# An fp32 latent-attention and mixture-of-experts layer: order of scores, mixing and statistics around the pairs

## The chip, the cores and the metric

The kernel runs on one core of one Trainium2 chip. The metric is device time of one execution in microseconds (us); the time given is the median of several runs.

## The reference

All numbers are fp32. `x` holds 32 batches of 32 latent rows of 512 values (1,024 rows); `ctx` holds 32 batches of 257 context rows of 384 values.

```python
h = LN(LN(x), g1, b1); c = LN(ctx, g2, b2)
q = h @ Wq + bq; k = c @ Wk + bk; v = c @ Wv + bv       # cross-attention, per batch
x = x + softmax(q @ k.T / sqrt(512)) @ v @ Wo + bo
h = LN(x)                                                # self-attention, per batch
q, k, v = three projections of h in 16 heads of 32 values; q, k = rope(q), rope(k)
x = x + concat(softmax(q @ k.T / sqrt(32)) @ v) @ Wo2.T + bo2
y = LN(x)
scores = sigmoid(y @ gate.T + bias)                      # 8 experts
share = the two best scores of a row / (their sum + 1e-6)
x = x + sum over the two of share * (silu(y @ w1[e].T) @ w2[e].T)
```

(Shortened: the kernel folds the key and value projections into the query and output weights, so that the context's normalisation reaches the scores as a factor per context row, the `rs` and `rx` below.)

## The kernel before

128 rows make a tile; there are eight tiles (groups, `g`) of four batches each, and four pairs of tiles (`p`). TensorE takes its instructions in the order in which the program is written. On VectorE (DVE), ScalarE (ACT) and GpSimd (POOL) a scheduler orders them by its own reckoning of when each can start; `tc.issue_after(x)` holds an instruction back until `x` in that reckoning. Each engine executes its own list in order. SyncE (SP) issues the loads and stores; POOL issues the indirect scatters.

The stages, with the profile's times:

1. Folding of weights (0 to 45 us).
2. Cross-attention, a loop over nine steps (45 to 139 us). A step `g` does `xmix_turn(g-1)` (transposes of the weights `ex`, tile `pte`, copied by ACT to `eT`, L628), `xscores(g)` (`pscore`, L580), `xmix(g-1)` (`pc` L637, then on DVE the mix `u`, L644), `xweights(g)` (transposes `prs` of the spread row factors `rx`, L595; scores times factors, exponentials), `cstats(g+1)` (eight `bn_stats` L528 on DVE, then `inverse` L510 to L518 on POOL, the last step a power that gives `rs`), `rspread(g+1)` (`rx`, an ACT copy, L564), `xout_turn(g-1)` (`ptu` L662), the queries of the next pair (`pq` L483 evacuated by ACT to `q2T` L487; `pbt` L475, copied to `pbs` L480, then `pb` L492), and `xout(g-1)` (`po` L671, residual sum L674). `cstats(g)` is held until the mix `u` of `g-2` (`pace["c", g]`).
   `load_ctx` brings the rows `n` of a group three steps ahead. Behind the last of them SP issues the four attention weights, and then a fill of `xs_d`, the experts' list in memory, with zeros (8 writes of 2,112 KB, L170).
3. Self-attention by pairs (139 to 303 us). For each pair: `scores` (`pqs`, 128 matmuls of 32 by 32, then maximum, subtraction and exponential), `shares` (sum, reciprocal, product, transposition into `aT`), `attend` (`pos`, 128 matmuls of 32 by 32, evacuated as `oT` L922, then `ppo` L934), `norm2`, the gate's logits, and for the pair before it `pick` (two best experts and shares) and `places` (positions in the experts' lists, `pi` L1068, and four scatters L1072 of rows to `xs_d`). `project` and `rotate` of the next pair lie between. `norm`, `xnorm` and `norm2` make `rs` by POOL's power and `nb`, minus mean times `rs`, on DVE.
   The last pair (250 to 303 us) has no next pair; `values(3,1)` (`ppv`), the sort of the experts by load (`order`) and the first expert's early work (`xse`, loaded from `xs_d` when the first three pairs' scatters have landed; transposes `xpe`, first matmuls `phe`) fill it.
4. The experts (303 to 540 us).

The order of the self-attention loop's start and of the last pair's start, before:

```python
# pair p of the loop (p = 0: no picks)
project(p + 1, 0, 0); shares(p, 0); scores(p, 1)
# picks of p - 1
project(p + 1, 0, 1); shares(p, 1); rotate(p + 1, 0); attend(p, 0)
project(p + 1, 1, 0); step(norm, p + 2); attend(p, 1)
# last pair
pick(p - 1); scores(p, 1); places(p - 1); values(p, (1,)); order(); attend(p, 0)
```

Of the kernel before, what the change touches and what calls it, by code (L numbers as in the profile page):

```python
# [1 line left out]

# [7 lines left out]
F32 = mybir.dt.float32  # L10
# [3 lines left out]
ALU = mybir.AluOpType  # L14
# [3 lines left out]
P = 128  # L18
# [34 lines left out]
def tile_perceiver_layer(  # L53
# [172 lines left out]
    with ExitStack() as attn:  # L226
# [19 lines left out]
        with ExitStack() as xa:  # L246
# [80 lines left out]
            def room(p, tag):  # L327
# [7 lines left out]
                    rooms[i // 4] = ewp.tile([P, KF * D], F32, tag="ew", name=f"pair{i // 4}")  # L335
                return rooms[i // 4][:, ts(i % 4, KD * N2)]

            def normalized(p, dsts):

                mv = spool.tile([P, 2, 2], F32, tag="mv2", name="mv2")  # L340
                for i in range(2):
                    stats_of(x_sb[:, 2 * p + i, :], mv[:, i, :])
                rs = rstd_of(mv, 2)
                nb = spool.tile([P, 2], F32, tag="nb", name="nb")
                nc.vector.scalar_tensor_tensor(
                    nb, mv[:, :, 0], -1.0, rs, op0=ALU.mult, op1=ALU.mult
                )
                for i in range(2):
                    nc.scalar.activation(
                        dsts[i], x_sb[:, 2 * p + i, :], AF.Identity,  # L350
                        bias=nb[:, i : i + 1], scale=rs[:, i : i + 1],
                    )
# [68 lines left out]
            def xnorm(p):  # L421

                mv = spool.tile([P, 2, 2], F32, tag="mv2", name="mv2")
                with tc.issue_after(pace["x", p]):
                    for i in range(2):
                        stats_of(x_sb[:, 2 * p + i, :], mv[:, i, :])

                ve = spool.tile([P, 2], F32, tag="ve2", name="ve")
                nc.vector.tensor_scalar(
                    ve, mv[:, :, 1], 1.0 + EPS, EPS * EPS, ALU.mult, ALU.add  # L430
                )
                rs = spool.tile([P, 2], F32, tag="rs2", name="rs")
                nc.gpsimd.tensor_tensor(rs, ve, mhalf[:, :2], ALU.pow)
                nb = spool.tile([P, 2], F32, tag="nb", name="nb")
                nc.vector.scalar_tensor_tensor(
                    nb, mv[:, :, 0], -1.0, rs, op0=ALU.mult, op1=ALU.mult
                )
                y = wk.tile([P, 2, D], F32, tag="y", bufs=1, name="y")
                for i in range(2):
                    nc.scalar.activation(  # L440
                        y[:, i, :], x_sb[:, 2 * p + i, :], AF.Identity,
                        bias=nb[:, i : i + 1], scale=rs[:, i : i + 1],
                    )
                qs[p]["y"] = y
# [61 lines left out]
            def inverse(st, m, n, tag):  # L506


                d = spool.tile([P, m], F32, tag="d" + tag, bufs=2, name="d9")[0:n]
                nc.gpsimd.tensor_tensor(d, st[:, :, 1], st[:, :, 4], ALU.subtract)  # L510
                nc.gpsimd.tensor_tensor(d, d, d, ALU.mult)
                v = spool.tile([P, m], F32, tag="v" + tag, bufs=2, name="v9")[0:n]
                nc.gpsimd.tensor_tensor(v, st[:, :, 2], st[:, :, 5], ALU.add)
                nc.gpsimd.tensor_scalar(d, d, DC / 4.0, EPS * DC, ALU.mult, ALU.add)
                nc.gpsimd.tensor_tensor(v, v, d, ALU.add)
                nc.gpsimd.tensor_scalar(v, v, 1.0 / DC, 0.0, ALU.mult, ALU.add)
                rs = spool.tile([P, m], F32, tag="rs" + tag, bufs=2, name="rs9")[0:n]
                nc.gpsimd.tensor_tensor(rs, v, mhalf[0:n, :m], ALU.pow)  # L518
                return rs

            def cstats(g):

                n = gs[g]["n"]
                st = spool.tile([P, 8, 6], F32, tag="st9", bufs=2, name="st9")

                with tc.issue_after(pace["c", g]):
                    for r in range(8):
                        nc.vector.bn_stats(st[:, r, :], n[:, r // 2, r % 2, :])  # L528
                gs[g]["rs"] = inverse(st, 8, P, "9")

            def lstats():
# [10 lines left out]
                nc.vector.tensor_reduce(  # L542
                    own[:, NTT:], eye.rearrange("p g b -> p b g"), AX.X, ALU.add
                )
                nc.vector.tensor_scalar_mul(own[:, 0:NTT], own[:, 0:NTT], rs)
                nc.vector.tensor_copy(
                    to.rearrange("p (b q) -> p b q", q=T),
                    own[:, NTT:].unsqueeze(2).to_broadcast([4 * NTT, 4, T]),
# [11 lines left out]
            def rspread(g):  # L560

                rs = gs[g]["rs"]
                rx = wk.tile([P, 2, 4, T], F32, tag="rx", bufs=1, name="rx")
                nc.scalar.copy(  # L564
                    rx,
                    rs[:, 0:8].rearrange("p (b c) -> p c b", c=2)
                    .unsqueeze(3).to_broadcast([P, 2, 4, T]),
                )
                rb = wk.tile([P, S], F32, tag="rb", name="rb")
                nc.scalar.copy(rb[:, NK : NK + 1], rlast[:, g : g + 1])  # L570
                gs[g]["rx"], gs[g]["rb"] = rx, rb
# [95 lines left out]
            def xout(g):  # L667
                uT = gs[g]["uT"]
                po = ps.tile([P, D], F32, tag="ps", name="po")
                for c in range(KC):  # L670
                    nc.tensor.matmul(  # L671
                        po, uT[:, c, :], wvo[:, c, :], start=(c == 0), stop=(c == KC - 1)
                    )
                nc.vector.scalar_tensor_tensor(  # L674
                    x_sb[:, g, :], po, gs[g]["rc"], x_sb[:, g, :],
                    op0=ALU.mult, op1=ALU.add,
                )


            DX = DC + 1  # L680
# [152 lines left out]
        with ExitStack() as sa:  # L833
# [16 lines left out]

            scatters = []
            cums = []
            def values(p, tiles=(0, 1)):
                for i in tiles:
                    v = wk.tile([P, D], F32, tag="v", bufs=4, name="v")
                    pp = ps.tile([P, D], F32, tag="ps", name="ppv")
                    for k in range(KD):
                        nc.tensor.matmul(  # L858
                            pp, st[p]["yT"][:, k, ts(i, P)], av[:, k, :],
                            start=(k == 0), stop=(k == KD - 1),  # L860
                        )
                    nc.scalar.copy(v, pp)
                    st[p]["v", i] = v

            def scores(p, i):

# [2 lines left out]
                for k in range(KD):  # L869
# [10 lines left out]
                mx = spool.tile([P, 4, KD], F32, tag="smx", name="smx")  # L880
                nc.vector.tensor_reduce(mx, sv, AX.X, ALU.max)
                ex = wk.tile([P, NH, T], F32, tag="sex", bufs=3, name="sex")
                nc.vector.tensor_tensor(
                    ex.rearrange("p (m k) s -> p m k s", k=KD),
                    sv,
                    mx.unsqueeze(3).to_broadcast([P, 4, KD, T]),
                    ALU.subtract,
                )
                nc.scalar.activation(ex, ex, AF.Exp, scale=ASCALE)
                st[p]["ex", i] = ex  # L890

# [97 lines left out]
            def pick(p):  # L989
# [25 lines left out]
                    )  # L1015
                nc.gpsimd.tensor_tensor(cc[:, 1, :], cc[:, 0, :], mk[:, 0, :], ALU.add)
                cums.append((cc, mk))

                sg = rt.tile([P, 2, 2], F32, tag="sg2", name="sg2")
                if p == NP - 1:  # L1020
                    nc.scalar.activation(sg, top[:, :, 0:2], AF.Sigmoid)
                else:
                    en = rt.tile([P, 2, 2], F32, tag="en", name="en")
                    nc.scalar.activation(en, top[:, :, 0:2], AF.Exp, scale=-1.0)
                    nc.vector.tensor_scalar_add(en, en, 1.0)
                    nc.vector.reciprocal(sg, en)
                den = rt.tile([P, 2], F32, tag="den", name="den")
                nc.vector.reduce_sum(den, sg, axis=AX.X)
# [7 lines left out]
                for i in range(2):  # L1036
# [3 lines left out]
                        y[:, i, YC : YC + NE], m[:, i, 1, :], c2[:, i, 1:2], cb,  # L1040
                        op0=ALU.mult, op1=ALU.add,
                    )
                st[p]["m"], st[p]["mk"], st[p]["cc"] = m, mk, cc

            def places(p):

                y, m, mk, cc = st[p]["fy"], st[p]["m"], st[p]["mk"], st[p]["cc"]
# [48 lines left out]
                nc.vector.tensor_copy(c, pn[:, 0:NE])  # L1096
                return c

            def order():

                full = [P, NE, NE]
                c = counts(cums[-1], "cnt0")
                key = keep.tile([P, NE], F32, name="key")
                nc.vector.scalar_tensor_tensor(
                    key, c, float(NE), down, op0=ALU.mult, op1=ALU.add
# [118 lines left out]
            def step(f, p, *a):  # L1224
                if 0 <= p < NP:
                    f(p, *a)
# [4 lines left out]
            for p in range(NP - 1):  # L1231
# [3 lines left out]
                    gate_turn(p - 1, 1)  # L1235
                project(p + 1, 0, 0)
                shares(p, 0)
                scores(p, 1)
                if p:
                    gate_logits(p - 1, 0)  # L1240
                    gate_logits(p - 1, 1)
                    pick(p - 1)
                project(p + 1, 0, 1)
                shares(p, 1)
                rotate(p + 1, 0)
                attend(p, 0)
                project(p + 1, 1, 0)
                step(norm, p + 2)
                attend(p, 1)
                if p:  # L1250
                    places(p - 1)
                project(p + 1, 1, 1)
                rotate(p + 1, 1)
                finish(p, 0)
                norm2(p, 0)
# [14 lines left out]
            shares(p, 0)  # L1270
            pick(p - 1)
            scores(p, 1)
            places(p - 1)
            values(p, (1,))
            order()
            attend(p, 0)
            shares(p, 1)
            finish(p, 0)
            norm2(p, 0)
# [8 lines left out]
            early_hidden(1)  # L1288
            gate_logits(p, 1)
            pick(p)  # L1290
            early_hidden(2)
            places(p)
            cnt = counts(cums[-1], "cnt")
# [343 lines left out]
```

## Time and profile before

| what | value |
|---|---|
| median of 9 runs | 552.15 us (550.63 to 556.8) |
| profiled execution | 551.48 us, span 549.8 us, mean granted TensorE clock 0.992 |
| TensorE busy | 515.4 us |
| VectorE busy | 242.2 us |
| ScalarE busy | 123.4 us |
| GpSimd busy | 105.9 us |
| DMA | 104.56 MB, mean 190 GB/s |

The profile is one execution. Busy time of TensorE is modelled from the starts of its matmuls. A row of the slices shows the span in 40 equal parts, each digit a busy share in tenths. A row of the waits names the waiting engine, tile and line, what released it, and the idle microseconds before it. A row of the timeline gives start, length, engine, line, operation, tiles (out<-in), and in brackets the idle time of the engine just before it with its releaser; "issue" there is idle time in which nothing that the profile shows was waited for.

### The profile page before, as it was taken

What the parts mean: (1) busy time and instruction counts of PE and PEld (TensorE: products, weight loads), DVE (VectorE), ACT (ScalarE), POOL (GpSimd) and SP (SyncE); (2) the same over time, 40 slices, a digit from 0 to 9 for tenths busy, and PEclk for the clock granted to TensorE, in tenths of its full rate; (3) what the DMA queues carried; (4) which work ended last, traced back from release to release, by engine and by line L of the source; (5) the groups of instructions that cost most, each with busy time, mean ns of one, the idle gap of its engine ahead of it and who ended that gap; (6) DMA issues with size and microseconds to landing.
All of it is one profiled execution on the core that took longest, in us unless ns stands there. A gap on an engine that the chain in (4) does not pass through costs nothing. (4 is left out here: it accounts for less than half of the span.)

```text
span 549.8 us, 11309 instructions
## 1 busy us (share of the span) xinstructions
PE 515.4 (94%) x4718; PEld 335.1 (61%) x4718; DVE 242.2 (44%) x706; ACT 123.4 (22%) x274; POOL 105.9 (19%) x185
## 2 busy tenths in 40 slices
PE   6999998999989999999899899999999999999991
PEld 3655454556665784876476366557566574868571
DVE  6564668655686575678651232113122121313110
ACT  3444444322311412312131021002011020102010
POOL 2323445220000013021302200131211202111202
PEclk9999999999999999999999999999999999999996
DMA  7999997999951002011594240936574436646512
GB/s 262 392 383 387 312 312 266 333 390 386 386 185 40 3 4 117 4 55 67 207 396 168 37 155 14 332 93 181 166 229 140 127 117 176 204 165 201 167 20 29
DMA packets 43647, 104.56 MB, mean 190 GB/s; under 512 B 4001, under 2 KB 7233, under 8 KB 42562
## 3 DMA queue, kind: packets, MB, share of 16 engines
q1 hardware_dynamic: 38994, 94.96, 48.3%
q0 software_dynamic: 4592, 8.78, 7.9%
q8 instruction: 39, 0.64, 0.5%
q14 instruction: 22, 0.18, 0.1%
HBM read 75.55 MB, written 28.18 MB: 189 GB/s over the span
## 5 line engine op out<-in xcount | busy, mean ns | idle before, releaser
L1402 PE MATMUL ph<-xT,w 128*128 128x288 f32 (+4 forms) x448 | 100.2, 382 | 3.1 <-ACT xT L177 3.1
L1402 PEld LDWEIGHTS ph<-xT,w 128*128 128x128 f32 x448 | 79.0, 190 | 19.6 <-ACT xT L177 3.7
L1464 PE MATMUL fpo<-w,hT 128*128 128x512 f32 x192 | 84.3, 595 | 0.0
L1464 PEld LDWEIGHTS fpo<-w,hT 128*128 128x128 f32 x192 | 35.9, 190 | 43.7 <-issue 43.5
L1408 DVE TENSOR_TENSOR hT<-ph,sg 128x288 f32<-128x288 f32 (+4 forms) x56 | 23.6, 422 | 62.9 <-ACT sg L1407 62.8
L1469 DVE TENSOR_SCALAR fob<-fpo,share 128x512 f32<-128x512 f32 x12 | 9.0, 751 | 76.5 <-PE fpo L1464 76.5
L1407 ACT ACTIVATE sg<-ph 128x288 f32<-128x288 f32 (+4 forms) x56 | 21.5, 384 | 85.0 <-PE ph L1402 81.3
L195 POOL DMA_INDIRECT out_dram<-fob,idx x12 | 18.6, 1548 | 103.2 <-DVE fob L1469 93.3
L528 DVE BATCH_NORM_STATS2 st<-n 128x6 f32<-128x384 f32 x64 | 32.7, 544 | 0.7 <-DMA n<-in_ctx_dram 0.6
L195 POOL DMA_INDIRECT out_dram<-fob,plc x9 | 13.9, 1547 | 91.6 <-DVE fob L1374 74.9
L177 ACT COPY xT<-xpt 128x512 f32<-128x512 f32 (+2 forms) x12 | 6.0, 497 | 112.5 <-PE xpt L1384 112.4
L934 PE MATMUL ppo<-ao,oT 128*128 128x512 f32 x64 | 28.5, 595 | 2.4 <-DVE oT L922 2.4
L671 PE MATMUL po<-wvo,uT 128*128 128x512 f32 x48 | 22.4, 602 | 1.2 <-ACT uT L664 1.2
L483 PE MATMUL pq<-x1T,mq 128*128 128x256 f32 x96 | 23.0, 384 | 0.0
L1072 POOL DMA_INDIRECT xs_d<-fy,pi x16 | 17.0, 1060 | 30.1 <-DVE pi L1068 20.2
L388 PE MATMUL pp<-syT,ak 128*128 128x256 f32 x96 | 22.4, 385 | 0.0
L1369 PE MATMUL fpq<-w,hT 128*32 128x128 f32 (+1 forms) x576 | 22.3, 309 | 0.0
L388 PE MATMUL pp<-syT,aq 128*128 128x256 f32 x96 | 22.1, 383 | 0.0
L934 PEld LDWEIGHTS ppo<-ao,oT 128*128 128x128 f32 x64 | 12.0, 190 | 15.8 <-issue 12.9
L858 PE MATMUL ppv<-av,syT 128*128 128x512 f32 x48 | 21.3, 594 | 0.0
L1369 PEld LDWEIGHTS fpq<-w,hT 128*32 128x32 f32 x576 | 16.3, 110 | 7.1 <-issue 3.2
L483 PEld LDWEIGHTS pq<-x1T,mq 128*128 128x128 f32 x96 | 17.4, 190 | 3.6 <-issue 1.2
(280 smaller groups left out, 734.1 us busy)
## 6 DMA issues: line engine op xcount, KB each, us to landing
xs_d<-zero SPq DMA_DIRECT2D x8, 2112.0 KB, 20.4
w<-in_w1T_dram SPq DMA_DIRECT2D x16, 1024.0 KB, 8.3
w<-in_w2T_dram SPq DMA_DIRECT2D x16, 1024.0 KB, 8.1
nT<-in_ctxT_dram SPq DMA_DIRECT2D x8, 1542.0 KB, 9.4
n<-in_ctx_dram SPq DMA_DIRECT2D x32, 384.0 KB, 7.2
xs<-xs_d SPq DMA_DIRECT2D x4, 528.0 KB, 9.2
x_sb<-in_x_dram SPq DMA_DIRECT2D x8, 256.0 KB, 6.6
out_dram<-x_sb SPq DMA_DIRECT2D x8, 256.0 KB, 2.9
```

The source lines that it names most:

```text
L195: return nc.gpsimd.indirect_dma_start(out=dst, out_offset=bass.IndirectOffsetOnAxis(ap=place, axis=0), in_=ob, in_offset=None, bounds_chec ...
L388: nc.tensor.matmul(pp[:, i, :], w[:, k, ts(e, P)], yT[:, k, :], start=(k == 0), stop=(k == KD - 1),)
L483: nc.tensor.matmul(pq[:, 0 : 2 * P], mq[:, k, ts(c, P)], x1T[:, k, :], start=(k == 0), stop=(k == KD - 1),)
L528: nc.vector.bn_stats(st[:, r, :], n[:, r // 2, r % 2, :])
L671: nc.tensor.matmul(po, uT[:, c, :], wvo[:, c, :], start=(c == 0), stop=(c == KC - 1))
L858: nc.tensor.matmul(pp, st[p]["yT"][:, k, ts(i, P)], av[:, k, :], start=(k == 0), stop=(k == KD - 1),)
L934: nc.tensor.matmul(pp, st[p]["oT", i][:, k].rearrange("p b q -> p (b q)"), ao[:, k, :], start=(k == 0), stop=(k == KD - 1),)
L1369: nc.tensor.matmul(po[ts(g, Q), 0:w], hT[:, f, ts(h, Q)], w2[:, f, ts(j, w)], start=(f == 0), stop=(f == KF - 1),)
L1402: nc.tensor.matmul(ph[:, 0:n], w1[:, k, ts(f, P)], t["xT"][:, k, 0:n], start=(k == 0), stop=(k == KD - 1),)
L1407: nc.scalar.activation(sg[:, 0:n], ph[:, 0:n], AF.Sigmoid)
L1408: nc.vector.tensor_mul(hT[:, f, 0:n], ph[:, 0:n], sg[:, 0:n])
L1464: nc.tensor.matmul(po, hT[:, f, ts(c, P)], w2[:, f, :], start=(f == 0), stop=(f == KF - 1),)
```

## The change

Five edits:

1. A helper `offsets` makes `nb` in `normalized` and `xnorm`: DVE negates the mean in place, POOL multiplies it by `rs`. Before, DVE did both in one instruction that read POOL's `rs`.
2. `inverse` loses its step `v * 1/DC`; the factor `DC ** 0.5` goes into the products that read `rs` (`own` on DVE, `rx` on ACT, now `nc.scalar.mul`).
3. In `cstats(g)` for `g >= 4`, three of the eight `bn_stats` are held only until the residual sum of `xout(g-3)`, and no longer until the mix of `g-2`.
4. First pair: `scores(0,1)` stands behind one more `project`, `attend(0,0)` and `attend(0,1)` each behind one more.
5. Last pair: `pick` is split in `pick` and `pick_shares`; the shares follow the second scores, and their first DVE step is held until the second subtraction. `values(3,1)` is split in halves; `places`, `counts` and `attend(3,0)` come between them, `order` behind them.

```diff
+            def offsets(mv, rs):
+                less = mv[:, :, 0]
+                nc.vector.tensor_scalar_mul(less, less, -1.0)
+                nb = spool.tile([P, 2], F32, tag="nb", name="nb")
+                nc.gpsimd.tensor_tensor(nb, less, rs, ALU.mult)
+                return nb
...
-                nb = spool.tile([P, 2], F32, tag="nb", name="nb")
-                nc.vector.scalar_tensor_tensor(
-                    nb, mv[:, :, 0], -1.0, rs, op0=ALU.mult, op1=ALU.mult
-                )
+                nb = offsets(mv, rs)
...
-                nc.gpsimd.tensor_scalar(v, v, 1.0 / DC, 0.0, ALU.mult, ALU.add)
...
-                with tc.issue_after(pace["c", g]):
-                    for r in range(8):
+                for r in range(8):
+                    soon = g >= 4 and r < 3
+                    with tc.issue_after(pace["r" if soon else "c", g]):
                         nc.vector.bn_stats(st[:, r, :], n[:, r // 2, r % 2, :])
...
-                nc.vector.tensor_scalar_mul(own[:, 0:NTT], own[:, 0:NTT], rs)
+                nc.vector.tensor_scalar(
+                    own[:, 0:NTT], own[:, 0:NTT], rs, DC ** 0.5, ALU.mult, ALU.mult
+                )
...
-                nc.scalar.copy(
+                nc.scalar.mul(
                     rx,
                     rs[:, 0:8].rearrange("p (b c) -> p c b", c=2)
                     .unsqueeze(3).to_broadcast([P, 2, 4, T]),
+                    DC ** 0.5,
                 )
...
-                nc.vector.scalar_tensor_tensor(
+                pace["r", g + 3] = nc.vector.scalar_tensor_tensor(
                     x_sb[:, g, :], po, gs[g]["rc"], x_sb[:, g, :],
                     op0=ALU.mult, op1=ALU.add,
-                )
+                ).ins
...
+            def pick_shares(p):
+                y, m, top = st[p]["fy"], st[p]["m"], st[p]["top"]
...
-                    nc.vector.tensor_scalar_add(en, en, 1.0)
+                    late = st[NP - 1].get(("less", 1))
+                    with tc.issue_after(late) if late else nullcontext():
+                        nc.vector.tensor_scalar_add(en, en, 1.0)
...
                 shares(p, 0)
-                scores(p, 1)
                 if p:
+                    scores(p, 1)
                     gate_logits(p - 1, 0)
                     gate_logits(p - 1, 1)
                     pick(p - 1)
+                    pick_shares(p - 1)
                 project(p + 1, 0, 1)
+                if p == 0:
+                    scores(p, 1)
                 shares(p, 1)
                 rotate(p + 1, 0)
-                attend(p, 0)
+                if p:
+                    attend(p, 0)
                 project(p + 1, 1, 0)
+                if p == 0:
+                    attend(p, 0)
                 step(norm, p + 2)
-                attend(p, 1)
                 if p:
+                    attend(p, 1)
                     places(p - 1)
                 project(p + 1, 1, 1)
+                if p == 0:
+                    attend(p, 1)
...
             pick(p - 1)
             scores(p, 1)
+            pick_shares(p - 1)
+            values(p, (1,), range(0, 2))
             places(p - 1)
-            values(p, (1,))
-            order()
+            n = counts(cums[-1], "cnt0")
             attend(p, 0)
+            values(p, (1,), range(2, KD))
+            order(n)
             shares(p, 1)
```

More of the change, by code (lines that the diff above doesn't have):

```diff
@@ L1 @@
-from contextlib import ExitStack
+from contextlib import ExitStack, nullcontext
 import concourse.bass as bass
@@ L433, in xnorm @@
                 nc.gpsimd.tensor_tensor(rs, ve, mhalf[:, :2], ALU.pow)
-                nb = spool.tile([P, 2], F32, tag="nb", name="nb")
-                nc.vector.scalar_tensor_tensor(
-                    nb, mv[:, :, 0], -1.0, rs, op0=ALU.mult, op1=ALU.mult
-                )
+                nb = offsets(mv, rs)
                 y = wk.tile([P, 2, D], F32, tag="y", bufs=1, name="y")
@@ L673, in xout @@
                     )
-                nc.vector.scalar_tensor_tensor(
+                pace["r", g + 3] = nc.vector.scalar_tensor_tensor(
                     x_sb[:, g, :], po, gs[g]["rc"], x_sb[:, g, :],
                     op0=ALU.mult, op1=ALU.add,
-                )
+                ).ins
             DX = DC + 1
@@ L852, in tile_perceiver_layer, with values @@
             cums = []
-            def values(p, tiles=(0, 1)):
+            def values(p, tiles=(0, 1), ks=range(KD)):
                 for i in tiles:
-                    v = wk.tile([P, D], F32, tag="v", bufs=4, name="v")
-                    pp = ps.tile([P, D], F32, tag="ps", name="ppv")
-                    for k in range(KD):
+                    if ks[0] == 0:
+                        st[p]["pv", i] = ps.tile([P, D], F32, tag="ps", name="ppv")
+                    pp = st[p]["pv", i]
+                    for k in ks:
                         nc.tensor.matmul(
@@ L861, in values @@
                         )
-                    nc.scalar.copy(v, pp)
-                    st[p]["v", i] = v
+                    if ks[-1] == KD - 1:
+                        v = wk.tile([P, D], F32, tag="v", bufs=4, name="v")
+                        nc.scalar.copy(v, pp)
+                        st[p]["v", i] = v
             def scores(p, i):
@@ L882, in scores @@
                 ex = wk.tile([P, NH, T], F32, tag="sex", bufs=3, name="sex")
-                nc.vector.tensor_tensor(
+                st[p]["less", i] = nc.vector.tensor_tensor(
                     ex.rearrange("p (m k) s -> p m k s", k=KD),
@@ L887, in scores @@
                     ALU.subtract,
-                )
+                ).ins
                 nc.scalar.activation(ex, ex, AF.Exp, scale=ASCALE)
@@ L1017, in pick @@
                 cums.append((cc, mk))
+                st[p]["m"], st[p]["mk"], st[p]["cc"], st[p]["top"] = m, mk, cc, top
+            def pick_shares(p):
+                y, m, top = st[p]["fy"], st[p]["m"], st[p]["top"]
                 sg = rt.tile([P, 2, 2], F32, tag="sg2", name="sg2")
@@ L1042, in pick @@
                     )
-                st[p]["m"], st[p]["mk"], st[p]["cc"] = m, mk, cc
             def places(p):
@@ L1097, in counts, with order @@
                 return c
-            def order():
+            def order(c):
                 full = [P, NE, NE]
-                c = counts(cums[-1], "cnt0")
                 key = keep.tile([P, NE], F32, name="key")
@@ L1290, in tile_perceiver_layer @@
             pick(p)
+            pick_shares(p)
             early_hidden(2)
```

## The prediction

> **What bounds the kernel now.** I read the page's busy times first, then the slices, then the waits of TensorE, and only then the timelines of the three places that the change touches.
>
> ```profile
> PE 515.4 (94%) x4718; PEld 335.1 (61%) x4718; DVE 242.2 (44%) x706; ACT 123.4 (22%) x274; POOL 105.9 (19%) x185
> DMA  7999997999951002011594240936574436646512
> ```
>
> TensorE is busy for 94% of the span, so nothing here can save much except by closing holes in its row. The DMA row says which holes may be tied to transfers: the 16 engines are full from the start to about 157 us, then nearly idle.
>
> ```profile
> PE prs L595 <- ACT rx L564: 4.0, 3, 1.4
> PE ppo L934 <- DVE oT L922: 2.4, 2, 1.6
> PE ptu L662 <- DVE u L644: 1.3, 2, 0.9
> PE pqs L873 <- issue: 1.2, 1, 1.2
> PE pos L915 <- issue: 0.9, 1, 0.9
> PE pmc L746 <- ACT trow L740: 0.6, 1, 0.6
> PE pr L1050 <- DVE sg L1026: 0.5, 1, 0.5
> ```
>
> Each line is: waiting matmul, what released it, us in total, times, longest. All seven are within the change's reach; together they are 10.9 us (2.0% of the span). That is the ceiling; the rest of the prediction asks how much of it is really collected. The experts' stage, 303 to 540 us, issues the same instructions in the same order before and after; I cost it at nothing, and so are the middle pairs, where the split of pick leaves the order as it was.
>
> **First pair: second scores and mixing behind projections (pqs, pos).**
>
> ```profile
> 152.29 0.55 PE L873 MATMUL pqs<-pair 32*32 32x32 f32 x41
> 154.01 0.94 PE L873 MATMUL pqs<-pair 32*32 32x32 f32 x87 [1.17 <-issue]
> 158.53 0.32 PE L915 MATMUL pos<-aT,v 32*32 32x32 f32 x25
> 159.74 1.07 PE L915 MATMUL pos<-aT,v 32*32 32x32 f32 x103 [0.89 <-issue]
> ```
>
> Columns: start, length, engine and line, then the idle time before it. In both groups of 128 small matmuls TensorE stops in the middle, for "issue", with all its data there. From the first stop to the second there are 87 small matmuls, 16 wide ones and 25 small ones: 128, each with its weight load, so 256 instructions. The instruction queue (q8 on the page) moves 16 KB packets at 151.45, 157.26 and 160.84, so a stop every 256 instructions is TensorE running out of code. Two groups of 128 tiny matmuls (10 ns each) use up a block in 1.3 us, while the zero fill of xs_d (its last landing is 160.29) holds the DMA engines that must bring the next one. In the changed order each group of small matmuls has one more wide group (16 matmuls, 3.72 us) ahead of it. The next block is then due 25 small matmuls into the second scores, at about 156.2, where before it was there by 154.0, and the one after it 9 into the first mixing, at about 161.0, when the fill has ended. So both stops should go: 1.17 + 0.89 = 2.06 us. If the second block is asked for at 156.4 and takes the 5.9 us that the one before took (148.0 to 154.0), it comes at 162.3, and up to 1.0 us of the second stop stays; with the DMA row falling to 3 and then 0 tenths there I keep 0.15. Term: **-1.9 us** (bounds -2.1 and 0).
>
> [...]
>
> **Cross-attention: statistics ahead of the mix, one POOL step less.** In inverse() one TENSOR_SCALAR goes; POOL's steps start 0.28 us apart (78.20 to 78.48), so every rs comes 0.28 us sooner. Twice in a row (lstats, then cstats(0)) that gives 0.56 of the 0.60 us that pmc waits for trow, which stands on ACT behind the first rx: -0.5 us. The first long wait of prs (71.53, 1.32 us) belongs to group 3, whose statistics don't move: -0.25.
>
> For groups 4 to 7 three of eight bn_stats (0.49 us apart, 1.46 together) go ahead of the mix's u, and the rest no longer stand behind the product of ex (0.4 to 0.6 us): rs comes 1.8 to 2.6 us sooner with the POOL step, I take 2.3 (rx becomes an ACTIVATE; q2T, an ACTIVATE of the same size, takes 0.47 where the copy took 0.40, which I count within this). But look at what ACT does with it:
>
> ```profile
> 75.79 0.47 ACT L487 ACTIVATE q2T<-pq,tcol 128x256 f32<-128x256 f32 x1
> 76.39 0.37 ACT L480 COPY pbs<-pbt 128x256 f32<-128x256 f32 x1
> 80.15 0.40 ACT L564 COPY rx<-rs 128x256 f32<-128x256 f32 x1 [3.39 <-POOL rs L518]
> 89.97 0.37 ACT L628 COPY eT<-pte 128x256 f32<-128x256 f32 x1 [0.37 <-PE pte L626]
> 93.59 0.40 ACT L564 COPY rx<-rs 128x256 f32<-128x256 f32 x1 [3.26 <-POOL rs L518]
> ```
>
> Now rx is last of its group and waits 3.39 us behind q2T and pbs. In the changed kernel, as it is built, rx stands ahead of q2T and pbs for groups 4 and 6, and ahead of eT for groups 5 and 7, because the scheduler reckons it ready sooner. ACT takes its instructions in order, so these copies wait for rx, and TensorE for them:
> - Group 4: rx at 80.15 - 2.3 = 77.85; q2T 0.31 later, pbs ends 0.84 after that, 79.0. The matmul pb ran at 78.08 without a wait, so it now waits about 1.1 us (0.2 of it is TensorE's own lead). +1.1.
> - Group 6: rx 102.91 - 2.3 = 100.6, pbs done at 101.75, pb was at 100.61: +1.0 after the lead.
> - Group 5: rx 91.3, eT done at 91.95, so pc starts at 92.05 instead of 91.18; prs follows it at 93.5 where it ran at 94.05 after its wait of 1.40: -0.5. The same for group 7 (rx 115.26, prs 115.71 after 1.33): -0.45.
> - nb: DVE no longer waits for POOL's pow (2.10 us at 94.26, 0.81 at 82.14, the latter followed by an nb of 1.23 us where others take 0.16). This is what ptu's 0.89 us comes from (u stood behind it): -0.4 of it, since u now has three bn_stats ahead of it instead (1.46 us, partly where the wait was). The price is eight POOL products of 0.2 us, right behind pow, and eight DVE products of 0.16 us; ACT's y and pair start at most 0.1 us later, beside a TensorE that has pq and po to do.
>
> Sum: -0.5 - 0.25 + 1.1 + 1.0 - 0.5 - 0.45 - 0.4 = **0.0 us**. The uncertain size is how much sooner rs comes; every 0.1 us of it is worth about 0.4 us over four groups (bounds -4.4 with rx out of the way, +2.8 if it gains 0.7 us less).
>
> On that nb of 1.23 us: it began at 82.14, beside a POOL addition that began at 82.07 and took 1.26. [...]
>
> **Last pair: shares behind the scores, mixing between.**
>
> ```profile
> 262.73 0.17 DVE L1068 CAST pi<-place 128x4 int32<-128x4 f32 x1
> 263.69 1.06 POOL L1072 DMA_INDIRECT xs_d<-fy,pi  x1 [3.53 <-DVE ssm L895]
> 276.46 0.22 DVE L1186 COPY_PREDICATED_SCALAR pl<-mask,xse 128x1 int32 x1 [2.67 <-DMA xse<-xs_d]
> ```
>
> TensorE waits here 0.45 (pr for sg), 0.81 and 1.56 (the two ppo for oT), 2.8 us in all, with the first mixing held up by two small gaps (1.84 us instead of 1.29). After the change attend(3,0) runs before the second half of values(3,1), so oT has 1.9 us of matmuls to hide in, its POOL scatters no longer lie across the mixing, and en + 1 stands behind the second subtraction, so the score chain (subtraction at 261.48) starts about 1.0 us sooner. Up to the second ppo that is 2.0 us. But pi, which every scatter reads, now comes behind the shares, counts and the keys of the order (some ten operations of 0.1 to 0.2 us, less the 0.68 us subtraction): about 0.6 us later. The scatters keep the 0.8 us from pi's end to their start, so xse lands at 277.05 instead of 276.45. The transposes xpe, which ran at 277.39 right behind ppo, would be due at 275.4 and wait until 277.15; gained so far 0.25. Behind them x_sb and its statistics are already done (they stood at 277.59 and 278.31, ahead of DVE's half of the copy xTe at 278.92), so that half comes 0.5 to 0.7 us sooner and phe, which waited 0.48, with it. Term: **-0.7 us** (bounds -2.0, xse no later, and +0.4, pi 1.2 us later).
>
> **Sum.** 0.0 - 1.9 - 0.7 = -2.6 us. The profiled execution took 551.48 us (span 549.8 and 1.7 around it), so its like would take 548.9; the median of the nine runs is 0.67 above it: 552.15 - 2.6 = **549.5 us**. What this kernel's measurement can tell from no change is about 0.5%, 2.76 us, so the forecast lies on that border.
>
> **Rivals.**
> - A, rx comes in time: rs gains over 3 us, and neither pb nor pc waits. Then the waits of prs go too (1.40 + 1.33), and with -0.5, -0.25, -0.9 the stage gives -4.4: 552.15 - 4.4 - 1.9 - 0.7 = 545.2. For it: rs's chain behind the last bn_stats is only 3.2 us. Against: five of eight bn_stats still follow u. Chance 0.12.
> - B, slower: rx blocks ACT for longer. Each us that rs comes later than I think costs 4 us (two pb, two pc). With rs only 1.65 us sooner instead of 2.3 the whole gain is gone; with 0.95 us sooner the time is 552.15 + 2.8 = 555. It decides where bn_stats in front of u wait on DVE for their rows n, which are in a saturated queue (n takes 7.2 us to land, up to 13.9). Chance 0.09.
> - C, the stops travel: TensorE runs dry in the new places as well, first-pair term zero: 551.4. For it: the fill's end is only 0.7 us before the second need. Chance 0.14.
> - D, the last pair's xse eats all, or the keys come earlier than I think: 550.2 or 548.2, inside the forecast's own range.
>
> **Numbers.** My forecast, with D in it, has 0.65, with a range of its own of 547.6 to 551.2, about half of it below 549.4. Faster by over 0.5%: 0.12 from A and 0.35 of the 0.65; slower by over 0.5%: half of B and a little for what no row shows, 0.08; between them 0.45. For 8 in 10 the low end goes part of the way to A (546.5), the high end past C to where B begins (552.5).
>
> **What would show it.** Right: no "issue" wait in pqs and pos of the first pair; prs no longer in the list, but pb and pc waiting for ACT pbs and eT, about 1 us each; xpe waiting for xse. Wrong: rx starting at once on ACT (then A), pb's waits of 2 us and more (B), a stop inside pqs or pos (C), xpe without a wait (last pair worth 2 us).

## The result, and the profile after

The changed kernel takes 559.15 us (median of 10 runs, 555.73 to 562.13), against 552.05 us of the kernel before beside it: ratio 1.012, 95% interval [1.0092, 1.0147]. I had forecast 549.5, with a range of 546.5 to 552.5. Its profiled execution has a span of 555.5 us, 5.7 more than before, and a mean granted clock of 0.985 (before 0.992). The medians lie 7.1 us apart; the other 1.4 us are in no trace. One run, of e7 below, took 1073.28 us and is left out of its ratio, though not of its median.

Waits of TensorE in the changed kernel, those that bear on the change, to be held against the seven lines shown before (waiting matmul, releaser, us in total, times, longest):

```profile
PE xpe L1197 <- DMA xse<-xs_d: 4.0, 1, 4.0
PE pc L643 <- ACT eT L634: 2.3, 3, 1.1
PE pb L494 <- ACT pbs L482: 1.9, 2, 1.0
PE pos L924 <- issue: 1.8, 1, 1.8
PE ppo L943 <- DVE oT L931: 1.6, 1, 1.6
PE prs L601 <- ACT rx L569: 1.0, 1, 1.0
PE ptu L668 <- DVE u L650: 0.7, 2, 0.4
PE pp L393 <- issue: 0.4, 1, 0.4
```

Of the seven waits that were named, those of prs, ppo and ptu are smaller and those of pqs, pmc and pr are gone; the stop of pos for issue, 1.8 us where it was 0.9, and the waits for xse, eT and pbs stand in their place. Pieces of TensorE's own time line show where the time went: the first matmuls of the self-attention begin at 146.66 (before 146.46, +0.2); the second pair's at 185.01 (182.90, +2.1); the last pair's second scores at 259.87 (257.95, +1.9); the first expert's transposes xpt at 317.78 (310.85, +6.9). From there on both kernels run alike. (The end of the span is 5.7 us later; 1.2 us are made up behind the last matmul.) So the cross-attention came out as forecast, the first pair lost 1.9 us where I had 1.9 as a gain, and the last pair lost 5.0.

In the cross-attention rx stands ahead of q2T and pbs on ACT, as read before the run; here for group 4, for which pb then waits 0.87 us:

```profile
77.01 0.41 ACT L569 ACTIVATE rx<-rs 128x256 f32<-128x256 f32 x1 [2.31 <-POOL rs L519]
77.33 0.46 ACT L489 ACTIVATE q2T<-pq,tcol 128x256 f32<-128x256 f32 x1
77.69 0.36 ACT L482 COPY pbs<-pbt 128x256 f32<-128x256 f32 x1
```

The first pair in TensorE's time line:

```profile
162.09 2.21 PE L393 MATMUL pp<-syT,ak 128*128 128x256 f32 x9
164.68 1.67 PE L393 MATMUL pp<-syT,ak 128*128 128x256 f32 x7 [0.38 <-issue]
166.28 1.22 PE L924 MATMUL pos<-aT,v 32*32 32x32 f32 x121
169.29 0.26 PE L924 MATMUL pos<-aT,v 32*32 32x32 f32 x7 [1.79 <-issue]
169.48 8.83 PE L943 MATMUL ppo<-ao,oT 128*128 128x512 f32 x16
```

The two stops that I had costed are gone, and the next two ends of a code block have stops instead, 0.38 + 1.79 us, 128 instruction pairs apart (7 + 121). And ppo takes 8.83 us where the same 16 matmuls took 7.03. The table by stretches tells why (columns: stretch, its length, busy us and instructions of TensorE, its loads, VectorE, ScalarE, GpSimd, then the granted TensorE clock, the DMA share, GB/s):

```profile
164.00:165.00 1.00, 0.62 (x4) 0.40 (x3) 0.97 (x3) 0.00 (x0) 0.00 (x0) 1.00 0.00 0
168.00:169.00 1.00, 0.00 (x0) 0.00 (x0) 0.55 (x1) 0.00 (x0) 0.00 (x0) 1.00 0.00 0
169.00:170.00 1.00, 0.71 (x8) 0.45 (x9) 0.39 (x1) 0.00 (x0) 0.00 (x0) 1.00 0.00 0
170.00:171.00 1.00, 1.00 (x3) 0.47 (x2) 1.00 (x2) 0.00 (x0) 0.00 (x0) 0.53 0.03 8
172.00:173.00 1.00, 1.00 (x2) 0.33 (x1) 0.97 (x2) 0.00 (x0) 0.00 (x0) 0.50 0.00 0
174.00:175.00 1.00, 1.00 (x4) 0.43 (x3) 0.09 (x1) 0.00 (x0) 0.00 (x0) 1.00 0.00 0
```

TensorE is granted half its clock for 3.41 us, from 170.07, 0.8 us after the second stop. The DMA share is near nothing during both stops, so the zero fill does not run beside them.

The last pair, on POOL, SP and TensorE:

```profile
266.03 1.06 POOL L1086 DMA_INDIRECT xs_d<-fy,pi  x1 [3.97 <-DVE ssm L904]
270.04 0.97 POOL L1086 DMA_INDIRECT xs_d<-fy,pi  x1 [0.30 <-issue]
```

```profile
269.56 0.42 SPq L1161 DMA_DIRECT2D w<-in_w1T_dram  x1
277.59 0.39 SPq L1168 DMA_DIRECT2D xse<-xs_d  x1
```

```profile
281.51 1.09 PE L1197 MATMUL xpe<-ident,xse 128*128 128x128 f32 x8 [4.02 <-DMA xse<-xs_d]
284.19 3.75 PE L1215 MATMUL phe<-xTe,w 128*128 128x256 f32 x8 [0.28 <-issue]
```

The first half of w1 (1,024 KB) is issued at 269.56, the fourth scatter at 270.04. Before, the scatter came first (267.62 against 268.41). In the packet records of the changed kernel w1's packets run from 271.3 to 275.0 and those of the fourth scatter from 274.4 to 276.9, 2.5 us instead of 0.8 to 1.1 for the other three; the scatter landed 7.3 us after its issue. SP issues xse when all scatters have landed, so at 277.59, and TensorE waits 4.02 us for it. Then eight phe take 3.75 us in place of 1.96:

```profile
281.00:282.00 1.00, 0.49 (x4) 0.49 (x5) 0.51 (x5) 0.00 (x0) 0.00 (x0) 1.00 1.06 414
284.00:285.00 1.00, 0.81 (x2) 0.75 (x3) 0.49 (x5) 0.00 (x0) 0.54 (x1) 0.50 1.03 385
288.00:289.00 1.00, 1.00 (x5) 0.93 (x4) 0.42 (x1) 0.47 (x2) 0.00 (x0) 0.50 1.08 408
290.00:292.00 2.00, 2.00 (x15) 1.87 (x14) 0.22 (x2) 0.38 (x1) 0.00 (x0) 1.00 1.01 401
```

Half clock again, for 6.83 us (282.71 to 289.53), after the longest wait. The kernel before has none at these places: eight ppo took 3.70 us there, sixteen 7.03 and eight phe 1.96.

### The profile page after: what moved, and what is told of

Read it like the earlier page. It is cut to its first block, busy times and chain, and to the rows that moved or that the text cites. A ratio compares the mean times of both kernels' runs of the same rounds, so it can differ in the third digit from the quotient of the medians.

```text
span 555.5 us, 11322 instructions
## 1 busy us (share of the span) xinstructions
PE 520.5 (94%) x4718; PEld 338.0 (61%) x4718; DVE 239.7 (43%) x706; ACT 122.6 (22%) x274; POOL 106.3 (19%) x184
## 5 line engine op out<-in xcount | busy, mean ns | idle before, releaser
L943 PE MATMUL ppo<-ao,oT 128*128 128x512 f32 x64 | 30.2, 625 | 1.6 <-DVE oT L931 1.6
```

What stands on the lines that cost most here:

```text
L943: nc.tensor.matmul(pp, st[p]["oT", i][:, k].rearrange("p b q -> p (b q)"), ao[:, k, :], start=(k == 0), stop=(k == KD - 1),)
```

## The experiments

My theory after the two traces had four parts: rx ahead of other copies on ACT eats the cross-attention's gain; code blocks come at a limited rate (packets of the instruction queue at 162.06, 166.69 and 171.48 in the changed kernel), so the stops of the first pair only move; w1 overtakes the fourth scatter; and an idle TensorE is followed by half clock, so that a wait costs up to twice its length (1.79 us of stop were followed by a loss of 1.8, 4.02 us by one of 2.8). The kernels were run in five groups ("call" in the expectations), each on one chip with the kernel before beside it. I name the groups by their chips: A (e1 to e4, kernel before 552.57), B (e5 to e8, 552.36), C (e9 to e12, 557.84), D (f0 to f3, 558.06), E (g1, g2, 558.35).

**The change in three parts (chip A).** e1 keeps the cross-attention edits, e2 the first pair's order, e3 the last pair's.

```diff
 # e1: offsets, inverse, own, rx, cstats as changed; the loop over pairs and the last pair as before
 # e2: only
-                scores(p, 1)                     # p = 0
...
+                if p == 0:
+                    scores(p, 1)
 # (and both attend(0, i) one project later)
 # e3: only pick / pick_shares, values in halves, counts and attend ahead of order
```

> Kernel before with the cross-attention edits alone (offsets, inverse without its last step, three bn_stats earlier, rx with the factor). In the changed kernel's trace the first matmuls of the self-attention come 0.21 us later than before. Theory (rx goes ahead of q2T, pbs and eT on ACT): the waits of prs go and pb and pc wait instead, 1.9 and 2.3 us in all; the time is that of the kernel before within 0.5 us (552). Rival (the edits bring the full 4 us of prs and the loss comes from elsewhere): 548.

> Kernel before with the first pair's order alone. Theory (TensorE's code comes in blocks of 256 instructions, one in 4.7 us at the soonest, whatever else the DMA engines do, and an idle stretch is followed by half clock): no stop in the second scores, but about 0.4 us in a later projection and 1.8 us in the second mixing, and where TensorE's clock halves after it another 1.8 us in ppo: 552 to 554. Rival (the stops come from the zero fill alone, as I predicted; the loss is the last pair's): both stops gone, 550.

> Kernel before with the last pair's order alone. Theory (the first expert's first half of w1 is issued before the fourth scatter and overtakes it, xse lands 4 us later, TensorE idles about 4 us and runs at half clock behind it): xpe waits about 4 us, time 556 to 558. Rival (the scatters are late only because pi is): xpe waits under 1 us, time 551 to 552.5.

Measured: e1 ratio 1.0009 [0.9981, 1.0037]; e2 1.0025 [0.9999, 1.0051]; e3 1.0069 [1.0041, 1.0098]. Together 1.03%, against 1.2% of the whole. In e1 prs waits 1.0 us and pb and pc 1.9 and 2.4, as the theory had it. In e2 the stops of the second scores are gone and pp and the second mixing stop for 0.28 and 1.56 us; its profiled execution kept the full clock there (1.00 from 168 to 174 us), so the pair takes 36.38 us, as before (36.44), while in the changed kernel's it takes 38.35. In e3 xpe waits 3.9 us for xse; the rival, by which only pi's delay makes the scatters late, expected under 1 us.

**Where code blocks end (chip B).**

```diff
+            pad = ps2.tile([P, D], F32, tag="pt", name="pad")
+            for _ in range(100):
+                nc.tensor.transpose(pad[0:Q, 0:Q], ident[0:Q, 0:Q], ident[0:Q, 0:Q])
             pms = [ps.tile([P, D], F32, tag="ps", name="pm") for _ in range(KD)]
```

> Changed kernel with 100 transposes of 32x32 that nobody reads put on TensorE between pmg and pm, where it waits 2.6 us for the weights anyway. Every later block of 256 TensorE instructions then begins 100 instruction pairs sooner in the program: 53 into the second scores of the first pair, 37 into its first mixing, 21 into its second. Theory (a block arrives every 4.7 us at most; now each holds 16 wide matmuls, 4.9 us of work): the waits of pos (1.8 us) and pp (0.4 us) for issue go, and the half clock behind them: 555 to 557. Rival (the small matmuls themselves stop, wherever the blocks begin): the same 1.8 us in the second mixing, 559.

Measured 559.76 (ratio 1.0129 [1.0102, 1.0156]): no gain in the sum, for two reasons outside the first pair. The 100 small transposes took 5.53 us (128 of the 32x32 matmuls of the scores take 1.29), which made everything after them 2.28 us later, and a stop of 2.16 us came up at a block's end in the fourth pair's scores. In the first pair the expectation held:

```profile
163.10 1.29 PE L927 MATMUL pos<-aT,v 32*32 32x32 f32 x128
164.31 3.72 PE L393 MATMUL pp<-syT,ak 128*128 128x256 f32 x16
167.96 1.29 PE L927 MATMUL pos<-aT,v 32*32 32x32 f32 x128
169.18 7.13 PE L946 MATMUL ppo<-ao,oT 128*128 128x512 f32 x16
```

The same instructions in the same order, without any stop, ppo at full clock, and the pair in 34.1 us instead of 38.35. So here the stops belong to the place where a block ends and not to the small matmuls, and the pair gains 2.4 us on the kernel before (36.44) only where no block ends badly. What moving the blocks would do for the order of before was not run.

**xse ahead of w1 (chip B).**

```diff
+                nc.sync.dma_start(xs, xs_d[...])
                 for h in range(2):
                     nc.sync.dma_start(w1[:, :, ts(h, D)], w1T[...])
-                    if h == 0:
-                        nc.sync.dma_start(xs, xs_d[...])
```

> Changed kernel with xse issued on SP ahead of the first half of w1 instead of behind it, all else in the same order. Theory (w1's 1,024 KB overtake the fourth scatter, whose landing xse waits for): the fourth scatter lands within 3 us, xse is issued near 274 instead of 277.6, the wait of xpe falls from 4.0 to about 1 us, w1 comes later and phe may wait up to 1.5 us for it; with less half clock 554 to 556. Rival (xse is late because pi and POOL's scatters are late): xse is issued as late as before, xpe still waits 4 us, 559.

Measured 553.86, ratio 1.0030 [1.0009, 1.0052]: 0.9 to 1.0% better than the changed kernel and e5. xse is issued at 272.82, xpe follows ppo without a wait and phe takes its normal time. (That xpe has no wait left is partly luck: the ppo before it ran at half clock here, 5.40 us instead of 3.70. In g2 and e9, with ppo at full clock (3.70 us), xpe waits 1.00 and 1.06 us, as expected.)

```profile
277.53 1.04 PE L1196 MATMUL xpe<-ident,xse 128*128 128x128 f32 x8
279.85 1.97 PE L1214 MATMUL phe<-xTe,w 128*128 128x256 f32 x8 [0.48 <-DVE mv L192]
```

From the second scores to the first expert the last pair takes 52.6 us (before 52.9, changed 57.9). The overtaking is the cause of the last pair's loss.

**rx behind eT (chip B).**

```diff
+                if 4 <= g < NTT:                  # after xmix_turn(g - 1)
+                    with tc.issue_after(gs[g - 1]["turned"]):   # its eT copy
+                        rspread(g)
...
-                        rspread(g + 1)
+                        if g + 1 < 4:
+                            rspread(g + 1)
```

> Changed kernel with rx of groups 4 to 7 held on ACT behind the eT copy of the group before, all else in the same order. Theory (rx ahead of pbs and eT on ACT is what eats the cross-attention's gain): the waits of pb (1.9 us) and pc (2.3 us) fall under 0.5 us each and prs stays under 1.5 us, so the self-attention begins 3.5 to 4 us sooner: 555. Rival (the statistics in front of u cost DVE as much): under 1 us gained, 558.5.

Measured 552.31, ratio 1.0000 [0.9976, 1.0024]: 1.2 to 1.3% better than the changed kernel, more than expected. The waits of pb are gone and the rest of pc and prs is small:

```profile
PE prs L601 <- ACT rx L569: 1.0, 1, 1.0
PE pc L643 <- ACT eT L634: 0.4, 1, 0.4
```

The self-attention begins at 143.09, 3.6 us sooner than in the changed kernel. That is what was expected of it. Of the other 3 us its profile puts 1.1 in the first pair (37.23 us instead of 38.35), where ppo kept the full clock this time; the rest I can't assign. xpe still waits 3.9 us there.

**All three on the changed kernel (chip B).**

> The three edits of the other runs together on the changed kernel: 100 small transposes at the start, xse ahead of w1, rx behind eT. If the three causes are separate, their gains add up: 559 - 3 - 4 - 4 = 548, under the kernel before. If they share the clock or the zero fill, less: 551.

Measured 551.29, ratio 0.9960 [0.9934, 0.9986]. A little faster than the kernel before, and faster than the changed one, but the transposes take back part of it (a stop of 2.44 us in the fourth pair, beside the 2.3 us at the start).

**Half clock by itself.** e4 (chip A) put four matmuls between ppo and xpe. The lines are those of f3 below, in which the tile comes from another pool.

```diff
+                warm = psq.tile([P, 4, KD, P], F32, tag="pq", name="warm")   # e4: from pool ps
+                for k in range(4):
+                    nc.tensor.matmul(warm[:, k % 4]..., ident, ao[:, k % KD, :], start=True, stop=True)
```

> Changed kernel with four matmuls of 128x128 by 512 that nobody reads, put on TensorE between the second ppo and the transposes xpe: 3.6 us of work in a stretch where it only waits. Theory (half clock follows an idle TensorE): the clock stays at 1.0 from 280 to 290 us and the time falls by about 3 us, to 556, though the wait for xse is as long. Rival (the clock falls for another reason, such as the loads of the weights): the time stays at 559.

Measured 559.03: no gain, and by itself no answer. The scheduler, reckoning with the longer TensorE, had put fy ahead of xTe on ACT, so that phe waited 2.2 us for xTe behind the warm matmuls, and the half clock came after that wait:

```profile
284.00:286.00 2.00, 0.00 (x0) 0.00 (x0) 1.31 (x7) 1.22 (x2) 0.55 (x1) 1.00 1.02 372
286.00:288.00 2.00, 1.88 (x5) 1.53 (x6) 0.17 (x1) 1.35 (x2) 0.00 (x0) 0.59 1.05 403
```

f3 (chip D) did it again, with fy and the last statistics held behind the xTe copies, and `early_turn` written ahead of `norm2`:

> Changed kernel with four matmuls of 128x128 by 512 that nobody reads between the second ppo and xpe, 3.6 us of work where TensorE waits for xse, and with fy and the last statistics held behind the xTe copies, so that ACT and DVE keep the order of the changed kernel. Theory (half clock follows the idle stretch): the clock stays at 1.0 from 280 to 290 us, phe takes 1.97 us for eight instead of 3.75, time 2.5 to 3 us under the changed kernel in the same call. Rival (the clock falls with the loads or the small matmuls): no difference.

Measured 556.18, against 558.64 for the changed kernel itself (f1) on that chip: 2.5 us, as the theory said.

```profile
276.89 3.60 PE L1198 MATMUL warm<-ao,ident 128*128 128x512 f32 x8
280.90 1.09 PE L1207 MATMUL xpe<-ident,xse 128*128 128x128 f32 x8 [0.42 <-DMA xse<-xs_d]
283.78 1.97 PE L1226 MATMUL phe<-xTe,w 128*128 128x256 f32 x8 [0.99 <-issue]
```

```profile
284.00:286.00 2.00, 2.00 (x12) 1.74 (x12) 0.65 (x5) 1.39 (x2) 0.36 (x1) 1.00 1.04 374
```

xse comes no sooner, TensorE does useless work, and the kernel is faster, because phe is at full clock: from xpe to the first poe TensorE takes 19.0 us, in f1 21.4. The loads fill the DMA engines as before (share 1.04), so they are not what halves the clock. What the holding alone would do was not run.

**Which parts are worth keeping (chip C).** e9 is the changed kernel with xse ahead of w1 and rx behind eT; e12 the same with the first pair as before; e10 has only the cross-attention edits with rx behind eT; e11 adds xse ahead of w1 to e10.

> Changed kernel with xse ahead of w1 and rx behind eT, without the small transposes (which cost 2.3 us at the start and brought a stop of 2.2 us in a later pair). If the two gains are separate: 552.3 - 5 = 547.5, faster than the kernel before. If the clock takes it back (each window of half clock costs up to 1.7 us): 550.

> Kernel before with the cross-attention edits and rx behind eT; both pairs as before. Theory (the cross-attention edits were worth 4 us, which rx ahead of pbs and eT ate): the self-attention begins 3 to 4 us sooner, 549. Rival (the early statistics bring nothing either way): 552.

> The same with xse ahead of w1, both pairs as before. In the kernel before the fourth scatter was issued 0.8 us before w1, so little should change: as the run without it, within 1 us. If w1 slows the scatters there too, 1 us faster.

> Changed kernel with xse ahead of w1 and rx behind eT, the first pair in the order of before. Theory (the first pair's edit moves the stops and gains nothing): within 1 us of the run with all edits. If the edit is a gain of 2 us by itself, 2 us slower than that run.

Measured: e9 548.45, ratio 0.9824 [0.9782, 0.9866]; e10 553.90, 0.9932 [0.9909, 0.9955]; e11 554.02, 0.9928; e12 549.77, 0.9847 [0.9797, 0.9898]. e10 gains 3.8 us, as expected of the cross-attention edits. e11 is equal to e10, e12 to e9 within their intervals; so the first pair's order gains nothing here (the pair takes 36.75 us in e9, 36.91 in e12). But the kernel before took 557.84 here, and e11 and e12, which differ in the last pair's order alone, lie 4.25 us apart. That called for the kernel before's own profile.

**The chip (D and E).** f0 is the kernel before, f1 the changed one, f2 and g1 are e9 again; g2 is the kernel before with the last pair's edits and xse ahead of w1.

> The kernel before, once more, for its profile on this chip. Ratio 1.000. If its time is near 558: stops of 0.3 to 0.5 us in pos while the scatters run, and half clock in the ppo behind them. If near 552: one or two stops of 0.2 us there.

> The changed kernel unaltered, beside the others of this call. On a chip where the kernel before takes 552 it should take 559 (ratio 1.012). If the small matmuls of the first mixing in the last pair stop beside the scatters on this chip as they did in the last call (3.4 us in eight stops, kernel before 557.8), the change saves that and the ratio should be near 1.00.

> The changed kernel with xse ahead of w1 and rx behind eT, unaltered from the last call, beside the others. If its gain over the kernel before was the edits' own: 547 to 548.5 whatever the chip, ratio 0.982 where the kernel before takes 558 and 0.992 where it takes 552.

> The changed kernel with xse ahead of w1 and rx behind eT, a third time. 547 to 548.5; ratio 0.992 if the kernel before takes 552 on this chip, 0.982 if it takes 558.

> Kernel before with the last pair's edits and xse ahead of w1, nothing else. Theory (the last pair's order is a gain where the scatters stop the small matmuls, and w1 ahead of the fourth scatter is its only cost): ratio 0.990 where the kernel before takes 558, 1.000 where it takes 552; xpe waits about 1 us. Rival (the later pi costs by itself): 2 us more than that.

Measured: f0 557.62, f1 558.64 (ratio 1.0011 [0.9990, 1.0032]), f2 547.83 (0.9815 [0.9789, 0.9840]), g1 547.43 (0.9813 [0.9784, 0.9842]), g2 551.76 (0.9888 [0.9857, 0.9920]). On chip D the change costs nothing, because the kernel before loses about as much in another way. The first mixing of the last pair in f0, beside the scatters:

```profile
266.65 0.57 PE L915 MATMUL pos<-aT,v 32*32 32x32 f32 x42
267.50 0.27 PE L915 MATMUL pos<-aT,v 32*32 32x32 f32 x4 [0.29 <-issue]
268.25 0.27 PE L915 MATMUL pos<-aT,v 32*32 32x32 f32 x4 [0.48 <-issue]
...
271.98 0.88 PE L915 MATMUL pos<-aT,v 32*32 32x32 f32 x63 [0.53 <-issue]
273.65 6.19 PE L934 MATMUL ppo<-ao,oT 128*128 128x512 f32 x8 [0.78 <-DVE oT L922]
```

Seven stops, 3.2 us, and then ppo at half clock (6.19 us instead of 3.70). In the profile before, this mixing took 1.84 us in all, 0.55 more than the second one. e10 and e11 on chip C, with the order of before, show the same as f0 (6.1 us for the mixing). With the last pair's order the mixing is over before the scatters begin, and takes 1.29 to 1.34 us on every chip.

## Why the prediction was wrong

- **Cross-attention, 0.0: held.** Measured +0.2. The start gave 0.51 (0.5 predicted); pb waits 0.87 and 1.03 (1.1 and 1.0); pc of group 5 starts at 91.80 (92.05); ptu's wait fell by 0.52 (0.4). The eight new DVE products took 0.15 to 0.16 us each, so none was held up as the one of 1.23 us had been. ACT's order, read before the run, was the right thing to read, and e7 shows the 3.6 us that it cost: near the forecast's rival A, at -4.4 for the stage.
- **First pair, -1.9: the step that failed is "and the one after it 9 into the first mixing, at about 161.0, when the fill has ended. So both stops should go".** The block ends lay where I had them (156.1 and 160.95), and both stops did go, but I followed the blocks no further, and took the fill for the only thing that limits them. It is not: with idle DMA engines the packets of the instruction queue start at 162.06, 166.69 and 171.48, and TensorE goes on at 164.68 and 169.29, each time 2.6 us after the packet. The block that begins 9 into the first mixing holds 119 small matmuls and 9 wide ones, 3.4 us of work, and the next one 7 wide and 121 small, 2.8 us; each is used up before its successor is there. Measured: stops of 2.06 us became 2.17, and half clock added 1.8. Rival C, which said so, had 0.14 and no price for the clock. How much work a block needs stays open: the kernel before ran through one of 3.2 us (164.44 to 167.65) without a stop, its packets only 3.5 us apart (160.84, 164.31). The fill seems to play a part where it still runs: in e9, with the self-attention 5 us sooner (DMA share 1.06 beside the second scores, from 150 to 152 us), a stop of 1.02 us is back in the first mixing. At 128 pairs a block the 4,718 pairs of the changed kernel would have some 37 block ends (an estimate); only these two show a stop for issue of more than 0.3 us.
- **Last pair, -0.7: the step that failed is "The scatters keep the 0.8 us from pi's end to their start, so xse lands at 277.05".** They kept it (0.81), and came 0.4 us later within the stage (0.6 predicted). But the keys came sooner, so w1's issue moved the other way, 0.8 us earlier within the stage, and passed the fourth scatter (e6 shows that this is the cause). I had costed what is moved on DVE and POOL and not SP's queue. The wait became 4.02 us where I had 1.75.
- **No term for the clock.** My sum took every us of idle TensorE at its face value. Of the last pair's 5.0 us 2.8 come behind the wait, at half clock (from xpe to the first poe 21.42 us instead of 18.62), of the first pair's 1.9 us 1.8: together 4.6 of the 5.7 us of the span. f3 gets 2.5 back though xse lands no sooner.
- Rival B had the right sign, but its mechanism, ACT held up for longer, did not occur: the waits of pb are those of the forecast.

## What to carry to other kernels

When a change moves instructions, follow every queue that they pass, the one that issues loads too: a small transfer that something waits for must not be started behind a big one that nobody needs yet (here 4.02 us of waiting for xse with w1's 1,024 KB in front, 1.00 in g2 and 1.06 in e9 with xse in front). Price a wait of TensorE at up to about twice its length, since half clock may follow it (here 1.56 us of waiting cost 1.7 more in e6, 1.79 cost 1.8, 4.02 cost 2.8), and look at the granted clock in the row behind it. Of stops for "issue" in runs of tiny matmuls count where the code blocks end (128 instruction pairs apart here), through the whole stretch and not only for the two that are seen; what is removed at one block's end can come back at the next (here 2.06 us of stops became 2.17).

The version with all edits, xse ahead of w1 and rx behind eT beats the kernel before on three chips (C, D, E; ratio 0.981 to 0.982, 547.4 to 548.5 us), and on D, the only one of them where it ran beside it, the changed kernel too. It was not measured on a chip where the kernel before takes 552; there e8, the same with the 100 transposes, has 0.9960.

## What the runs showed of the hardware that I had not expected

- On chip A the spread of the kernel before goes with the granted clock: 549.08 us at a mean of 0.994, 555.8 at 0.982. Of the dips to half clock, five inside the work were measured from start to end: 3.41 and 6.83 us in the changed kernel, 3.4 in e4, 6.8 in e2 and 6.8 in f1.
- What sets off a dip was not found. The same wait of ppo, 1.56 us, was followed by half clock in e6 (eight ppo 5.40 us) and not in the changed kernel (3.70). A stop of 1.79 us, behind 1.2 us of 32x32 matmuls, was followed by it in the changed kernel, and the stop at the same place in e2 (1.56 us) was not; in e2 the clock was at 0.50 to 0.51 from 260 to 266 us behind pg (128x8) and pqs (32x32) with no wait over 0.5 us. Whether the tiny matmuls have a part in it was not tried by itself.
- In its stops at block ends TensorE went on 2.5 to 2.6 us after the packet of the next block began (2.56 and 2.48 in the kernel before, 2.62 and 2.60 in the changed one). Around these places the packets were 3.5 to 4.8 us apart with the DMA engines idle (160.84, 164.31 and 168.17 in the kernel before; 162.06, 166.69 and 171.48 in the changed one), and 5.8 us with the fill running (151.45 and 157.26, and 151.56 and 157.34). What sets the distance was not found.
- Small matmuls stopped for 0.3 to 0.5 us at a time while POOL issued indirect scatters on chips C, D and E (3.2 us in f0, 0.5 in g2), and hardly on A and B (the mixing of e1 takes 1.85 us beside them). What differs was not found; each chip ran one group only, so chip and group can't be told apart.
